# A planned scan layer: numbers per batch, measured durations, paired silus, and six small loads moved to mid-layer

## The chip, the cores and the metric

The kernel runs on one core of a Trainium2 chip, as one launch. The metric is the device time of a launch in microseconds (us). A core has five engines with their own instruction streams: PE (TensorE, matmuls and transposes), DVE (VectorE), ACT (ScalarE, functions from a loaded table), POOL (GpSimd) and SP (SyncE, which here issues nearly all DMAs). Each runs its instructions in order and waits on semaphores for the others. All data is fp32.

## The reference

Two layers, each with a residual, on x of 4 x 512 x 32 x 32 (a batch is 512 channels by 1024 tokens; gn is a group norm with 32 groups):

```
# layer 0, a selective scan over the 1024 tokens of each batch
xn   = layer_norm(gn(x) as tokens x channels) * ln_w + ln_b
xm,z = split(xn @ W_in)                       # 1024 channels each
xs   = silu(causal_conv4(xm) + conv_b)
dt,B,C = split(xs @ W_x); dt = softplus(dt @ W_dt + b_dt)
h[t] = exp(dt[t]*A) * h[t-1] + (dt[t]*xs[t]) * B[t]   # 16 states per channel, A = -exp(A_log)
y[t] = sum over states of h[t]*C[t]
x    = x + ((y + D*xs) * silu(z)) @ W_out
# layer 1, position attention with two 3x3 convolutions
g    = gn(x)
top, center = 1x1 convs(g) with b_top, b_center; bottom = 3x3 conv(g) + b_bottom
m    = softmax over all of (center^T @ top)
x    = x + (3x3 conv(g + m @ bottom) + b_out)
```

## The kernel before

**Tiling of the scan layer.** A batch's 1024 tokens are two halves of 512; its 1024 inner channels are eight chunks of 128 partitions, taken in four pairs. One stretch is a pair and a half (function `delta` makes dt, dt*x and its transpose), and has 16 units, one per state (function `unit`). So a batch has 8 stretches and 128 units, the layer 4 batches and 512 units. One unit, for both chunks of the pair:

- the decay exp(dt*A), on ACT (L862, 128x512 each);
- the input term dt*x*B, in one of two ways. A unit "on ACT" scales rows of the transposed dt*x by B (L875, `sc`, four instructions of 128x256) and PE turns them into PSUM (L901, tile `u`); the decay goes to SBUF (`da`). Otherwise POOL multiplies dt*x by a broadcast B (L890, `dbx`), and the decay goes to `u`;
- the scan over 512 tokens on DVE (L915);
- the product with a broadcast C, on POOL for both chunks at once (L938), or on DVE for each (L931) in some of the units that are not on ACT;
- the sum over states: PE adds the transposed products in PSUM (L948, tile `y`).

After 16 units `gate` multiplies by silu(z) and writes a product to DRAM, and `out_proj` (for the last batch `last_proj`) projects it and adds x. The rows of B and C come as DMAs that broadcast 2 KB to 128 partitions (`bbc`, three buffers; `cbc`, five buffers), issued by SP.

**Which units go where.** `shares` reads two tables: ACT_B, the number of units on ACT in each stretch, and DVE_C, the number that DVE multiplies by C. Each has three rows: batch 0, batches 1 and 2, batch 3.

**What runs in between.** While a batch is scanned, `project_batch` makes the next one ready: `norms` (both norms), `conv1` for each chunk (PE's projection `pxm`, ACT's first tap L667, DVE's other taps L676, then silu on ACT, L685), `params` (dt, B and C). `gates` makes silu(z) (L739). `transform` turns a piece of the second layer's 3x3 weights on POOL (18 pieces, three loads, two scalings on ACT at L1200 and L1201, five kinds of POOL step, twelve stores). Batch 0 is made half by half (`conv1_half`).

**Tables on ACT.** silu, softplus and exp (with log) are in three table sets. A step whose set isn't the loaded one makes ACT load it first (ACT_TABLE_LOAD; for exp it is written at L210).

**What sets the order.** All of this is a list of steps with an engine, an assumed duration, a due time (`prio`, counted in units), what they read, write and hold, and perhaps a table. `Plan.issue` keeps a clock for each engine and always issues the step that could start first, among those within SLACK of it the one due first. A step in another table is held back, by 5.46 table loads, unless it is due well ahead of the rest. HOP and LAG are assumed delays between engines, AHEAD how far past the earliest open due time an engine may go. Due times are numbers in `PRM`: when the projections, gates and pieces fall due. The order so made is the program's order on each engine; the planner's clock has no other effect.

**Ahead of the plan**, in program order: SP loads `gm_sb` and the four chunks of the first x (L294); POOL's queue loads the second layer's `wt_sb` (two DMAs) and `pb_sb` (two); ACT's queue loads `brow_b` and `brow_o`, the second layer's two biases, through a view whose last dimension has stride (L233), and ACT scales them by -12 (L236). Then ACT's queue loads the first layer's small inputs (L315: lnw, lnb, cw, cb, bdt, dp, a_sb), wx and wdt; ACT takes exp of a_sb (L327) and DVE negates it (L328). The first norm is `bn_stats` and `bn_aggr` on DVE (L446, L447), a matmul with gm_sb (L454), small DVE steps, a second matmul (L470), and log and exp on ACT (L479, L484).

**The second layer** (L1324 and later) is written without the planner: scores (L1364, L1385), two 3x3 convolutions as transformed products (L1533), attention (L1585).

Of the kernel before, what the change touches and what calls it, by code (L numbers as in the profile page):

```python
# [8 lines left out]
F32 = mybir.dt.float32  # L9
# [21 lines left out]
PRM = dict(tf=-22.1, pg=0.35, kt=2.5, ke=2.06, ka=-1.93, fl=0, fi=-4.54, m0=42.67, n0=49.76, nl=1.48, q0=67.23, qg=4.59, c0=60.23, cg=6.17, p0=114.55, e0=1.02, eg=7.73, g0=80.83, gg=9.09, o0=14.49, og=6.33, dl=12.15, t0=8, tg=57.65)  # L31


ACT_B = ((12, 9, 10, 9, 9, 10, 9, 9), (11, 9, 12, 8, 9, 8, 8, 8), (9, 9, 12, 12, 11, 12, 12, 13))
DVE_C = ((4, 7, 5, 1, 2, 3, 5, 5), (4, 3, 3, 2, 1, 5, 2, 4), (4, 4, 4, 4, 3, 1, 4, 2))
# [24 lines left out]
class Plan:  # L60
# [4 lines left out]
    LAG = {"PE": 0.2, "DVE": 0.08, "ACT": 0.1, "POOL": 0.06, "SP": 0.0}  # L65
    HOP, LOAD, SLACK, AHEAD = 0.05, 1.3, 0.11, 15.09
# [41 lines left out]
    def issue(self):  # L108
        ready = {e: [s for s in self.steps if s.eng == e and not s.unmet] for e in self.ENGINES}
        clock = {e: 0.0 for e in self.ENGINES}  # L110
# [4 lines left out]
        while left:  # L115
# [4 lines left out]
            for e in self.ENGINES:  # L120
                urgent = min((s.prio for s in ready[e] if s.table in (None, table)), default=1e9)
                found = []
                for s in ready[e]:
                    if s.prio > last:
                        continue
                    t = max(clock[e], s.ready)
                    for b in s.takes:
                        turn = b.free or b.ring not in queues or queues[b.ring][0] is b
                        t = max(t, min(free[b.ring])) if free[b.ring] and turn else 1e9
                    if t >= 1e9:  # L130
                        continue
                    late = s.table not in (None, table)
                    wait = t + (5.46 * self.LOAD if late and s.prio > urgent - 2.66 else 0.0)
                    found.append((wait, s.prio, t, late, s))
# [24 lines left out]
            for b in s.bufs:  # L159
                b.left -= 1  # L160
                if b.ring and not b.left:
                    free[b.ring].append(s.done + self.HOP)
                    if b.done:
                        b.done(b.tile)
            ready[s.eng].remove(s)
            for u in s.users:
                u.unmet -= 1
                other = u.eng != s.eng or s.kb
                u.ready = max(u.ready, s.done + self.HOP if other else clock[s.eng])
# [6 lines left out]
def mamba_then_pab_kernel(  # L176
# [46 lines left out]
    nc.gpsimd.dma_start(wt_sb[:, :, 0, :], w_top.rearrange("(c p) n -> p c n", p=P))  # L223
    nc.gpsimd.dma_start(wt_sb[:, :, 1, :], w_center.rearrange("(c p) n -> p c n", p=P))
    pb_sb = cpool.tile([P, 1], F32, tag="pb", name="pb_sb")
    nc.gpsimd.dma_start(pb_sb[0:PAB], b_top)
    nc.gpsimd.dma_start(pb_sb[PAB:P], b_center)


    brow = []  # L230
    for name, src in (("b", b_bottom), ("o", b_out)):
        t = cpool.tile([1, C], F32, tag=f"brow_{name}", name=f"brow_{name}")
        nc.scalar.dma_start(  # L233
            t.rearrange("o (c p) -> o c p", p=P), src.rearrange("p (c o) -> o c p", o=1)
        )
        nc.scalar.activation(t, t, AF.Copy, scale=-12.0)  # L236
        brow.append(t)
# [46 lines left out]
    with ExitStack() as l0:  # L284
# [7 lines left out]
        first_x = xtp.tile([P, NCC, L], F32, tag="xt", name="xt_0", bufs=1)  # L292
        for c in range(NCC):
            nc.sync.dma_start(first_x[:, c, :], x[0, c * P : (c + 1) * P].rearrange("p h w -> p (h w)"))  # L294

# [6 lines left out]
        def shares(b, n):  # L302

            k = min(b, 1) + (b == B - 1)
            rest = NS - ACT_B[k][n]
            off = [int((i + 0.5) * (NS - 1) / rest) for i in range(rest)]
            c = DVE_C[k][n]
# [20 lines left out]
        nc.vector.tensor_scalar_mul(a_sb, a_sb, -1.0)  # L328
# [39 lines left out]
        MM, TR = 0.88, 0.114  # L368
        ROWS, EXP, SCAN = 0.8, 0.61, 1.18
# [49 lines left out]
        def norms(b, prio, lag=0.0):  # L419

            t = xts[b] = buf("xt", [P, NCC, L], f"xt_{b}")
            if b == 0:
                t.make = lambda: first_x
            src = x[b].rearrange("(c p) h w -> p c (h w)", p=P)
            xin = [buf(None, None, "") for c in range(NCC)]
            step("SP", 0.0, lambda: t(), [], [], prio, holds=[t])
            for c in range(NCC):
                step(
                    "SP", 0.3,
                    lambda c=c: b and nc.sync.dma_start(t()[:, c, :], src[:, c, :]),  # L430
                    [], [xin[c]], prio, kb=512, holds=[t],
                )
# [6 lines left out]
            for c in range(NCC):  # L439
# [9 lines left out]
                step("DVE", 1.4, stats, [xin[c]], [stat], prio, holds=[t])  # L449
# [15 lines left out]
            step("DVE", 0.6, mid, [], [pm, stat], prio)  # L465
# [47 lines left out]
            step("PE", 0.6, shift_mean, [stat], [pv], prio)  # L513
# [61 lines left out]
            for h, (r, pvar) in enumerate(zip(rs, pvars)):  # L575
                at = prio if b else at_half[h]
                step(
                    "ACT", 0.58,
# [74 lines left out]
        def conv1(b, d, prio):  # L653
# [5 lines left out]
            for at, end in ((0, 341), (341, 682), (682, L)):  # L659
# [22 lines left out]
                step("DVE", 0.25 + n * 0.0042, taps, [p], xsh, prio, holds=[u])  # L682
            step(
                "ACT", 1.06,
                lambda: nc.scalar.activation(u(), u(), AF.Silu, bias=cb_sb[:, d : d + 1]),  # L685
                [], xsh, prio, "silu", holds=[u],
# [40 lines left out]
        def gates(b, d, prio):  # L727
# [3 lines left out]
            for h, hs in enumerate(halves):  # L731
                p = project(b, NDC + d, w, f"pz_{b}_{d}_{h}", hs, prio)
                step(
                    "ACT", 0.48,
# [12 lines left out]
        def params(b, prio, hh=tuple(range(NH))):  # L747
# [4 lines left out]
            for n, h in enumerate(hh):  # L752
                hs = halves[h]
                pp = buf("mm" if b or h else "y0", [P, T], f"pp_{b}_{h}")
                for d in range(NDC):
# [7 lines left out]
                        prio + PRM["pg"] * (d + NDC * n) if b else prio - 0.05 * (NDC - d),  # L763
                        holds=[xs[b, k] for k in range(NDC)] if (b or h) and d == 0 else [xs[b, d]],
                    )
                end = prio + (PRM["pg"] * NDC * (n + 1) if b else 0)
                step(
                    "ACT", 0.48,
# [26 lines left out]
        def delta(b, e, h, prio):  # L795
# [5 lines left out]
            for j in range(2):  # L801
# [4 lines left out]
                    "ACT", 0.58,  # L806
# [23 lines left out]
            for j in range(2):  # L830
                pt = buf("mm", [P, NK, P], f"pdt_{name}_{j}")

                def turn(j=j, pt=pt):
# [5 lines left out]
                    "ACT", 0.48, lambda j=j, pt=pt: nc.scalar.copy(dtxt()[:, :, j, :], pt()),  # L839
# [4 lines left out]
        def unit(b, e, h, s, y):  # L844
# [50 lines left out]
            for j, u in enumerate(us):  # L895
                part = parts[j]
                if on_act:
# [11 lines left out]
                    step("PE", 4 * TR, turn, [sc], [u], prio - PRM["kt"])  # L909
                else:  # L910
                    step("ACT", EXP, lambda j=j, u=u: decay(j, u()), [dt], [u], prio - PRM["ke"], "exp")

                def scan(j=j, u=u):
# [10 lines left out]
                    "DVE", SCAN + 0.14 if h == 0 and on_dve else SCAN, scan,  # L924
# [3 lines left out]
                if on_dve:  # L928
                    step(
                        "DVE", 0.6,  # L930
# [3 lines left out]
            if not on_dve:  # L934
                def times_c():
# [5 lines left out]
                    "POOL", 2.31 if h else 2.5, times_c,  # L941
                    [c_bc], [*parts, *([] if h else carry[s])], prio, holds=[hc],
                )
            for j in range(2):
# [8 lines left out]

                step("PE", 4 * TR, add, [parts[j]], [y[j]], prio - PRM["ka"], holds=[hc])

        def gate(b, e, h, y):
# [12 lines left out]
            for j in range(2):  # L969
                step(  # L970
                    "ACT", 0.48, lambda j=j: nc.scalar.copy(yt()[:, j], y[j]()),
                    [y[j]], [yt], prio - 0.5,
                )
            for j in range(2):
# [19 lines left out]
                step("DVE", 1.39, mul, [uh, sz], [p, uh if kept else sz], prio + 2, holds=[u])  # L994
# [111 lines left out]
        def first_image(prio):  # L1106
# [50 lines left out]
            step("DVE", 0.6, mid, [], [pm, stat], prio)  # L1157
# [83 lines left out]
        def project_batch(b):  # L1241

            at = (b - 1) * NDC * NS
            norms(b, at + (PRM["m0"] if b == 1 else PRM["n0"]), PRM["nl"])
            for d in range(NDC):
                when = at + (PRM["q0"] + PRM["qg"] * d if b == 1 else PRM["c0"] + PRM["cg"] * d)
                conv1(b, d, when)
            params(b, at + PRM["p0"])

        norms(0, -20)  # L1250
        for d in range(NDC):
            conv1_half(d, 0, -17 + 0.1 * d)
        params(0, -16, (0,))
        for k in range(NPC + EARLY):
            u, src = ((ub, w_bottom), (uo, w_out))[k // NPC]
            transform(u, src, k % NPC, -5 if k < PRM['t0'] else PRM['tf'] + PRM['tg'] * (k - PRM['t0']))

        LAST = {
            3: (range(4), range(NH), 128 * (B - 1) + 70, 8),
            5: (range(4, 6), range(NH), 128 * (B - 1) + 104, 3),  # L1260
            6: (range(6, NDC), (0,), 128 * (B - 1) + 117, 2),
            7: (range(6, NDC), (1,), 128 * B, 2),
        }
        for b in range(B):
            at = b * NDC * NS
            for n in range(NDC):
                e, h = divmod(n, NH)
                delta(b, e, h, (at + n * NS - PRM["dl"], -15, 9.6)[0 if b else {0: 1, 1: 2}.get(n, 0)])
                if b == n == 0:
                    for d in range(NDC):  # L1270
                        conv1_half(d, 1, -4 + 1.5 * d)
                    params(0, 8.6, (1,))
                if n == 0:
                    for k in range(NDC):
                        gates(b, k, (PRM["e0"] + PRM["eg"] * k, at - 128 + PRM["g0"] + PRM["gg"] * k)[min(b, 1)])
                    if b:
                        for k in range(NH):
                            out_proj(b - 1, k, at + PRM["o0"] + 4 * PRM["og"] * k, PRM["og"])
# [9 lines left out]
        with tc.manual_schedule():  # L1288
            plan.issue()

# [452 lines left out]
```

## Time and profile before

| | us |
|---|---|
| median of 3 runs (lowest, highest) | 2928.78 (2926.93, 2932.84) |
| the profiled execution's own time | 2926.95 |
| its span, first to last instruction | 2925.1 |
| PE busy, all | 2724.9 |
| DVE busy, all | 2292.1 |
| ACT busy, all | 1831.1 |
| POOL busy, all | 2045.6 |
| table loads on ACT: L210 (67), L813 (32), L739 (29), L685 (21), L723 (4) | 1.283 each |

A page of the profile covers one execution. "Busy" is time in which an engine ran instructions; waits, branches and the issuing of DMAs are not counted, and a DMA's issue shows under a queue's name (SPq, ACTq). A group row gives how often a kind of instruction ran, its busy time in all, the mean of one, and the idle time just before it with what ended that. Where instructions overlap in the pipeline, busy time over count is less than the mean of one. A stretch of the timeline gives the start of a row, its length, and in brackets the idle time before it. The granted clock of PE was 0.985 of full speed over the span.

### The profile page before, as it was taken

The page shows a single profiled execution, that of the slowest core. Times are in us where ns is not written, and L with a number is a line of the kernel's source. Part 1 is how long each engine was busy: PE and PEld are TensorE (multiplying, and loading weights), DVE is VectorE, ACT ScalarE, POOL GpSimd, SP SyncE. Part 2 cuts the span into 40 slices and gives each one's busy share as a digit, 9 for nine tenths or more (in the row PEclk, how much of TensorE's full clock was granted, in tenths as well). Part 3 has the DMA queues.
Part 4 walks back from the last instruction along what each step waited for, and adds up shares of the span by engine and source line. Part 5 has one row for each costly group of instructions (what it writes and reads, how often), then busy time and mean ns, then how long its engine had stood idle before and what let it go on. Part 6 is the DMA issues. An engine that isn't in the chain of part 4 may idle for free.

```text
span 2925.1 us, 36166 instructions
## 1 busy us (share of the span) xinstructions
PE 2724.9 (93%) x11712; PEld 1615.4 (55%) x11712; DVE 2292.1 (78%) x2719; ACT 1831.1 (63%) x3248; POOL 2045.6 (70%) x1247
## 2 busy tenths in 40 slices
PE   5988899999899999899999989799999999999998
PEld 2456566666666666666656666544444444444444
DVE  4679899988999989999979999867776655346254
ACT  4689899998799999889998999630200003030000
POOL 6899898899998999998999999733141341214222
PEclk9999899999999999999999999999999999999999
DMA  6856555467545577655567654757789886536487
GB/s 168 235 155 199 165 158 166 152 213 242 195 140 165 172 213 246 200 150 152 175 204 216 219 172 147 160 217 263 256 277 290 307 329 242 200 124 236 162 319 259
DMA packets 405348, 603.94 MB, mean 206 GB/s; under 512 B 46088, under 2 KB 245000, under 8 KB 380584
## 3 DMA queue, kind: packets, MB, share of 16 engines
q1 hardware_dynamic: 396352, 587.11, 62.5%
q10 hardware_dynamic: 8648, 14.26, 1.4%
q8 instruction: 94, 1.54, 0.2%
q14 instruction: 94, 0.77, 0.1%
q0 software_dynamic: 160, 0.26, 0.0%
HBM read 504.53 MB, written 96.99 MB: 206 GB/s over the span
## 4 chain that ended last, share of the span: by engine, by line
PE 34%; DVE 7%; POOL 6%; ACT 5%; issue 3%; DMA 2%; SPq 0%; DVEq 0%; POOLq 0%; ACTq 0%
PE m_o L1533 11%; PE m_b L1533 8%; PE pat L1585 6%; POOL da L938 2%; PE y L948 2%; PE po L412 2%; DVE da L915 2%; PE u L901 1%; ACT sc L875 1%; PE psc L1385 1%; ACT da L862 1%; POOL dbx L890 1%; DMA uw_o<-u_o 1%; POOL dbx L938 1%; DMA u_o<-wr 1%
## 5 line engine op out<-in xcount | busy, mean ns | idle before, releaser
L938 POOL TENSOR_TENSOR da<-da,cbc 128x1024 f32<-128x1024 f32 x313 | 739.9, 2369 | 46.1 <-DVE da L915 32.8
L875 ACT ACTIVATE sc<-dtxt,bt_sb 128x256 f32<-128x256 f32 x1252 | 550.5, 498 | 22.6 <-PE u L901 21.6
L890 POOL TENSOR_TENSOR dbx<-dtx,bbc 128x1024 f32<-128x1024 f32 x199 | 469.9, 2371 | 26.5 <-PE y L948 12.9
L862 ACT ACTIVATE da<-dt,a_sb 128x512 f32<-128x512 f32 x626 | 431.2, 713 | 25.4 <-PE y L948 24.4
L915 DVE TENSOR_TENSOR_SCAN da<-da,u 128x512 f32<-128x512 f32 x328 | 383.8, 1203 | 26.2 <-PE u L901 16.9
L901 PE MATMUL u<-ident,sc 128*128 128x128 f32 x2504 | 363.0, 277 | 34.1 <-DVE da L915 13.8
L948 PE MATMUL y<-ident,da 128*128 128x128 f32 x2504 | 348.8, 279 | 48.9 <-POOL da L938 45.8
L901 PEld LDWEIGHTS u<-ident,sc 128*128 128x128 f32 x2504 | 293.5, 142 | 168.3 <-issue 64.3
L915 DVE TENSOR_TENSOR_SCAN da<-da,carry_sb,u 128x512 f32<-128x512 f32 x298 | 365.2, 1259 | 19.8 <-PE u L901 15.6
L948 PEld LDWEIGHTS y<-ident,da 128*128 128x128 f32 x2504 | 287.7, 143 | 132.3 <-POOL da L938 101.6
L1533 PE MATMUL m_o<-uw_o,v_o 128*128 128x512 f32 x768 | 336.4, 597 | 8.3 <-DMA uw_o<-u_o 8.2
L1533 PE MATMUL m_b<-uw_b,v_b 128*128 128x512 f32 x768 | 333.7, 593 | 4.8 <-ACT e_b L1541 2.2
L862 ACT ACTIVATE u<-dt,a_sb 128x512 f32<-128x512 f32 x398 | 264.9, 681 | 13.9 <-DVE da L915 8.9
L412 PE MATMUL pxm<-xt,winc 128*128 128x345 f32 (+3 forms) x704 | 240.9, 485 | 11.2 <-DMA winc<-in_w_in_dram 4.0
L1533 PEld LDWEIGHTS m_o<-uw_o,v_o 128*128 128x128 f32 x768 | 145.3, 191 | 190.9 <-issue 179.8
L1533 PEld LDWEIGHTS m_b<-uw_b,v_b 128*128 128x128 f32 x768 | 144.9, 190 | 189.9 <-issue 178.9
L412 PE MATMUL pz<-xt,winc 128*128 128x512 f32 x512 | 244.0, 596 | 6.0 <-DMA winc<-in_w_in_dram 2.0
L948 PE MATMUL y<-ident,dbx 128*128 128x128 f32 x1592 | 221.0, 276 | 8.7 <-POOL dbx L938 7.3
L938 POOL TENSOR_TENSOR dbx<-dbx,cbc 128x1024 f32<-128x1024 f32 x93 | 220.6, 2372 | 10.7 <-DMA bbc<-bcd 5.4
L1585 PE MATMUL pat<-y_b,st 128*128 128x512 f32 x512 | 223.3, 597 | 1.6 <-DVE rz L1594 1.6
L948 PEld LDWEIGHTS y<-ident,dbx 128*128 128x128 f32 x1592 | 183.3, 142 | 49.5 <-POOL dbx L938 19.6
L1541 ACT ACTIVATE e_o<-m_o 128x512 f32<-128x512 f32 x24 | 14.3, 597 | 276.8 <-PE m_o L1533 276.8
(229 smaller groups left out, 4259.2 us busy)
## 6 DMA issues: line engine op xcount, KB each, us to landing
cbc<-bcd SPq DMA_DIRECT2D x512, 256.0 KB, 3.7
uw_b<-u_b SPq DMA_DIRECT2D x96, 1024.0 KB, 4.8
uw_o<-u_o SPq DMA_DIRECT2D x96, 1024.0 KB, 4.8
bbc<-bcd SPq DMA_DIRECT2D x199, 256.0 KB, 4.0
u_b<-work SPq DMA_DIRECT2D x192, 128.0 KB, 2.8
winc<-in_w_in_dram SPq DMA_DIRECT2D x72, 256.0 KB, 3.9
szd<-sz SPq DMA_DIRECT2D x32, 512.0 KB, 3.6
szl<-szd SPq DMA_DIRECT2D x32, 512.0 KB, 5.1
```

The lines of the kernel that those rows point to most:

```text
L412: lambda k=k, lhs=lhs, rhs=rhs: nc.tensor.matmul(p()[:, at : at + cols], lhs(), rhs(), start=(k == 0), stop=(k == n - 1)),
L862: nc.scalar.activation(t, dt()[:, j], AF.Exp, scale=a_sb[:, at : at + 1])
L875: nc.scalar.activation(sc()[:, k], dtxt()[:, k], AF.Copy, scale=bt[:, at, s : s + 1])
L890: lambda: nc.gpsimd.tensor_mul(hc(), dtx(), b_bc().to_broadcast([P, 2, T])),
L901: nc.tensor.transpose(u()[:, k * P : (k + 1) * P], sc()[:, k, j, :], ident)
L915: nc.vector.tensor_tensor_scan(ht, *((hc()[:, j], u()) if on_act else (u(), hc()[:, j])), carry_sb[:, j, s : s + 1] if h else 0.0, ALU.mul ...
L938: nc.gpsimd.tensor_mul(hc(), hc(), c_bc().to_broadcast([P, 2, T]))
L948: nc.tensor.matmul(y[j]()[:, k, :], hc()[:, j, k * P : (k + 1) * P], ident, start=(s == 0 and k == 0), stop=(s == NS - 1 and k == NK - 1), ...
L1385: nc.tensor.matmul(pt, top[:, m * P : (m + 1) * P], center[:, h * T : (h + 1) * T], start=True, stop=True,)
L1533: nc.tensor.matmul(m[q], v[:, q, k, c, :], w[:, c, :], start=(c == 0), stop=(c == NCC - 1 and not extra),)
L1541: nc.scalar.activation(e, m[2], AF.Copy, scale=al / 2)
L1585: nc.tensor.matmul(pt, st[m][:, 2 * P * j + h : 2 * P * (j + 1) : 2], xb[m // 2][:, m % 2, :], start=(m == 0), stop=(m == NMC - 1),)
```

## The change

1. The three rows of ACT_B and DVE_C become four, one for each batch, with other numbers, and PRM has values per batch for most due times; the due times of the 18 weight pieces are written out.
2. The planner's assumed durations, hops and lags get other values, hops one per engine; its clocks start at BEGIN instead of zero; the hold on a step in another table goes from 5.46 to 2.11 loads.
3. `silus` becomes a step of its own, for one or two chunks: two in batches 1 and 2, one in batch 3.
4. `wt_sb`, `pb_sb` and the two brows are loaded by a step of SP with due time 300 (a batch is 128), and the brows are scaled after the plan in the program's text, outside its fixed order; in the order that results, these two instructions stand on ACT in the third stretch of batch 2.
5. The first x is loaded by the plan's steps (due at -100); a_sb is negated on ACT.

```diff
-ACT_B = ((12, 9, 10, 9, 9, 10, 9, 9), (11, 9, 12, 8, 9, 8, 8, 8), (9, 9, 12, 12, 11, 12, 12, 13))
-DVE_C = ((4, 7, 5, 1, 2, 3, 5, 5), (4, 3, 3, 2, 1, 5, 2, 4), (4, 4, 4, 4, 3, 1, 4, 2))
+ACT_B = (
+    (12, 8, 10, 9, 10, 8, 8, 8),
+    (11, 8, 12, 9, 8, 9, 8, 8),
+    (11, 9, 13, 9, 10, 8, 9, 9),
+    (9, 11, 12, 12, 10, 13, 12, 14),
+)
+DVE_C = (
+    (3, 5, 6, 3, 1, 3, 5, 6),
+    (4, 7, 2, 3, 3, 5, 2, 5),
+    (5, 4, 3, 1, 5, 6, 3, 6),
+    (4, 3, 3, 4, 6, 1, 3, 1),
+)
...
-    LAG = {"PE": 0.2, "DVE": 0.08, "ACT": 0.1, "POOL": 0.06, "SP": 0.0}
-    HOP, LOAD, SLACK, AHEAD = 0.05, 1.3, 0.11, 15.09
+    LAG = {"PE": 0.17, "DVE": 0.095, "ACT": 0.1, "POOL": 0.06, "SP": 0.0}
+    HOP = {"PE": 0.16, "DVE": 0.045, "ACT": 0.06, "POOL": 0.08, "SP": 0.05}
+    BEGIN = {"PE": 5.0, "DVE": 1.5, "ACT": 9.0, "POOL": 7.0, "SP": 1.5}
+    FREE, LOAD, SLACK, AHEAD = 0.06, 1.3, 0.11, 15.44
+    TURN, URGENT = 2.11, 2.89
...
-                    wait = t + (5.46 * self.LOAD if late and s.prio > urgent - 2.66 else 0.0)
+                    wait = t + (self.TURN * self.LOAD if late and s.prio > urgent - self.URGENT else 0.0)
...
-    nc.gpsimd.dma_start(wt_sb[:, :, 0, :], w_top.rearrange("(c p) n -> p c n", p=P))
-    nc.gpsimd.dma_start(wt_sb[:, :, 1, :], w_center.rearrange("(c p) n -> p c n", p=P))
...
-        nc.scalar.activation(t, t, AF.Copy, scale=-12.0)
-        brow.append(t)
+    def load_l1():
+
+        for k, w in enumerate((w_top, w_center)):
+            nc.sync.dma_start(wt_sb[:, :, k, :], w.rearrange("(c p) n -> p c n", p=P))
+        nc.sync.dma_start(pb_sb[0:PAB], b_top)
+        nc.sync.dma_start(pb_sb[PAB:P], b_center)
+        for t, src in zip(brow, (b_bottom, b_out)):
+            nc.sync.dma_start(
+                t.rearrange("o (c p) -> o c p", p=P), src.rearrange("p (c o) -> o c p", o=1)
+            )
...
-        nc.vector.tensor_scalar_mul(a_sb, a_sb, -1.0)
+        nc.scalar.activation(a_sb, a_sb, AF.Copy, scale=-1.0)
...
-            step(
-                "ACT", 1.06,
-                lambda: nc.scalar.activation(u(), u(), AF.Silu, bias=cb_sb[:, d : d + 1]),
-                [], xsh, prio, "silu", holds=[u],
+        def silus(b, ds, prio):
+
+            def several():
+                for d in ds:
+                    u = xs[b, d]
+                    nc.scalar.activation(u(), u(), AF.Silu, bias=cb_sb[:, d : d + 1])
+
+            step(
+                "ACT", 1.06 * len(ds), several, [], [t for d in ds for t in xh[b, d]], prio, "silu",
+                holds=[xs[b, d] for d in ds],
             )
...
                 conv1(b, d, when)
-            params(b, at + PRM["p0"])
+                if (d + 1) % PRM["xp"][b - 1] == 0:
+                    silus(b, range(d + 1 - PRM["xp"][b - 1], d + 1), when)
+            params(b, at + PRM["p0"][b - 1])

         norms(0, -20)
+        step("SP", 1.6, load_l1, [], [], 300, kb=64)
...
         with tc.manual_schedule():
             plan.issue()
+        for t in brow:
+            nc.scalar.activation(t, t, AF.Copy, scale=-12.0)
```

The rest of the diff is the numbers of PRM (among them xp=(2, 2, 1), the pairing by batch) and the durations handed to `step`, such as SCAN 1.18 to 1.12 or DVE's taps 0.0042 to 0.0037 us per element.

## The prediction

> **What bounds the kernel now.** I read the page's slices first, then the busy time by stretch, cut where the last scan of each batch ends. Those ends I found by laying the planner's order of scans beside the trace: 592, 1042, 1503 and 1883 us. Columns: length, then busy time of PE, its weight loads, DVE, ACT and POOL.
>
> ```profile
> core 0: us, PE busy (x) PEld busy (x) DVE busy (x) ACT busy (x) POOL busy (x), PEclk, DMA share, GB/s
> 0.00:592.00 592.00, 514.72 (x2494) 324.84 (x2495) 483.64 (x607) 506.34 (x872) 508.88 (x357) 0.97 0.59 174
> 592.00:1042.00 450.00, 422.80 (x2300) 288.29 (x2299) 410.95 (x474) 413.80 (x725) 422.38 (x254) 0.98 0.61 188
> 1042.00:1503.00 461.00, 432.06 (x2335) 295.20 (x2334) 413.81 (x477) 424.92 (x741) 435.05 (x267) 0.99 0.61 188
> 1503.00:1883.00 380.00, 344.74 (x2144) 253.40 (x2143) 368.20 (x398) 349.01 (x670) 373.63 (x230) 0.99 0.62 190
> 1883.00:2925.00 1042.00, 1010.61 (x2448) 453.67 (x2446) 615.47 (x766) 137.05 (x242) 305.61 (x143) 0.99 0.71 247
> ```
>
> Four engines are nearly equal in the first layer; POOL is the fullest of the elementwise ones in every batch, and in the last batch it hardly idles (374 of 380). The second layer (last row) is PE's, 1011 of 1042 us, and its code is the same. So the change is worth what it does to the 1883 us ahead of it. There the loss is largest at the start, which the timeline shows (start, duration, engine, line, what; idle time before in brackets):
>
> ```profile
> 0.76 1.26 ACTq L233 DMA_DIRECT2D brow_b<-in_b_bottom_dram  x1
> 2.05 2.44 ACTq L233 DMA_DIRECT2D brow_o<-in_b_out_dram  x1
> 4.52 8.45 ACTq L315 DMA_DIRECT2D lnw_sb<-in_ln_w_dram  x1
> 13.79 1.28 DVE L446 BATCH_NORM_STATS2 bs_l<-xt 128x6 f32<-128x512 f32 x2 [0.62 <-DMA xt<-in_x_dram]
> 14.76 1.35 SPq L1195 DMA_DIRECT2D work<-in_w_bottom_dram  x2
> ...
> 19.69 0.23 DVE L328 TENSOR_SCALAR a_sb<-a_sb 128x128 f32<-128x128 f32 x1 [4.62 <-ACT a_sb L327]
> 19.84 0.20 DVE L447 BATCH_NORM_AGGREGATE mv_l<-bs_l 128x2 f32<-128x12 f32 x1
> 20.09 0.59 PE L454 MATMUL pm_l<-mv_l,gm_sb 128*128 128x4 f32 x2 [20.09 <-DVE mv_l L447]
> ...
> 24.04 0.52 ACT L1200 ACTIVATE work<-work 128x384 f32<-128x384 f32 x1 [4.38 <-DMA work<-in_w_bottom_dram]
> ...
> 26.29 0.27 ACT L479 ACTIVATE gdev_l<-pv_l,eps 128x4 f32<-128x4 f32 x1
> ```
>
> x is there by 13.8 us, yet the first norm goes on at 26.3. Behind the two brow loads lnw's issue takes 8.45 us. Behind that come a_sb, its exp on ACT and its negation on DVE (L328), which stands ahead of the last aggregate. SP's first weight piece also waits for lnw (its queue's waits put 8.4 us down to it), so ACT's L1200, ahead of L479, runs at 24.04.
>
> The rows that cost the edits (count, busy us, mean ns):
>
> ```profile
> L938 POOL TENSOR_TENSOR da<-da,cbc 128x1024 f32<-128x1024 f32 x313 | 739.9, 2369 | 46.1 <-DVE da L915 32.8 <-POOL carry_sb L937 0.2
> L875 ACT ACTIVATE sc<-dtxt,bt_sb 128x256 f32<-128x256 f32 x1252 | 550.5, 498 | 22.6 <-PE u L901 21.6
> L890 POOL TENSOR_TENSOR dbx<-dtx,bbc 128x1024 f32<-128x1024 f32 x199 | 469.9, 2371 | 26.5 <-PE y L948 12.9 <-DMA bbc<-bcd 7.0 <-DVE xs L676 3.4
> L931 DVE TENSOR_TENSOR dbx<-u,cbc 128x512 f32<-128x512 f32 x212 | 138.6, 670 | 0.0
> L685 ACT ACT_TABLE_LOAD x21 | 26.9, 1283 | 0.4
> ```
>
> **The change part by part.** Both kernels can be counted without running, from the order in which the planner issues.
>
> *Shares (ACT_B, DVE_C).* Units that ACT feeds go from 313 to 317 (77, 73, 73, 90 by batch to 73, 73, 78, 93). Those that DVE multiplies by C go from 106 to 121 (32, 24, 24, 26 to 32, 31, 33, 25). POOL loses 4 dbx products and 15 products by C net, 19 x 2.37 = 45 us, and 7 carry copies of 0.19: -46. DVE gains 30 products of 0.65 (138.6/212) and 14 carry copies of 0.16: +22. ACT gains 16 sc of 0.44 (550.5/1252): +7. PE gains 32 transposes of 0.145 (363.0/2504 of L901): +5.
>
> *Silus of two convolutions in one step.* The order holds 141 table loads instead of 153: silu of conv1 21 to 14, of the gates 29 to 26, the rest -2. By the trace one costs 1.28 us, and the next ACTIVATE starts 0.02 us later (98.10 + 1.28, then 99.40): 12 x 1.3 = -15.6 us of ACT. The Trainium skill (ScalarE: Activation LUTs, "What ACT_TABLE_LOAD costs") adds a drain of about 1.38 us and gives 2.66 per switch, which would make -32. The drain would have to stand ahead of the load; there the ACTIVATE ends at 98.09 and the load starts at 98.10. I take the trace. ACT in sum: about -8. A pair also holds the first silu back until the second convolution's taps are done; these xs are for the next batch, a cover of tens of us, and if it were gone params would wait some 5 us once per batch.
>
> *Totals up to the last scan* (order times row): POOL 1739 to 1694, ACT 1694 to 1686, DVE 1676 to 1696, PE 1652 to 1656. The fullest engine falls from 1739 to 1696: -43, if work can move freely over the layer. The fullest by batch is 509, 423, 430, 377 before and 516 (POOL), 420 (DVE), 435 (PE), 369 (DVE) after: 1739 to 1740, no gain, if each batch keeps its idle time. Cut finer, into the 32 stretches of 16 units, the sum of each one's fullest engine goes from 1841 to 1836. Measured is 1883, so neither end is reached. Engines do run ahead over a batch's end (next batch's convolutions, deltas, and up to five loads), and POOL, the one relieved, is the one that idles least; but the other three are close behind. I take half of 43: -21.
>
> *Start.* brow leaves the ACT queue, the negation goes to ACT (+0.3, in its idle time), and SP's first two weight pieces go ahead of x. x then lands at about the same time (0.39 MB more ahead of it, 2.3 us at the slice's 168 GB/s; 0.26 MB of wt and the brow gone). L447 can follow at about 15.5 instead of 20.0, pv 2 us later; ACT's L1200 still stands ahead and now waits for the third piece, behind x and two winc loads, 16 to 18.5 us; table load 1.3; L479 at 18 to 20.5 instead of 26.3. From 46 to 100 us PE is the bound (busy 18 to 19 of every 20 us), and it waits for this chain, so most of it carries on, less a second pair of weight scalings between the first squares. I take -7 (bounds -11 and 0: POOL's pieces may not start earlier).
>
> *Small loads in mid-layer.* Six DMAs are put in SP's queue in the second stretch of batch 2, ahead of the loads of C for unit 0 of the third. The wt and pb loads took 1.06 + 0.80 + 0.58 + 0.54 to issue on POOL, the brows 1.26 + 2.44 on ACT, and whatever stood next 8.45: 15 us for the queue if it repeats. The Trainium skill (DMA: Bandwidth & Descriptors, "Rules for kernel authors") says why and speaks against this place: a last dimension that isn't contiguous becomes one descriptor per element, so each brow's 2 KB are 512 of them, wherever they are issued; sized by bytes alone (260 KB at 188 GB/s) the six would cost 1.4 us. Cover: cbc has five buffers, 5 x 2.9 us = 14.4 (a stretch of 16 units is 46 us), less 3.7 for landing. So 0 to 5 us of bubble on DVE and POOL; on ACT the two scalings of brow now stand between sc and decays of that stretch, some 12 us later, and wait up to 2 if the landing takes the 13 us of the start. I take +4, bounds 0 and 15. At the start the removal is in the -7.
>
> *HOP, LAG, BEGIN, TURN, due times of pieces, projections, gates:* they cost no instruction, they set the order. Their worth is what they do to idle time. The idle rows are many small ones (longest single wait in the four batches 10.1 us), so I can bound it only by POOL's idle outside the start, (592 - 509 - 34) + 28 + 26 + 6 = 109 us: 30 less or 15 more. I take 0 beyond the half above. Second layer: 0.
>
> Sum: -21 - 7 + 4 = -24 on the profiled execution's own 2926.95 (span 2925.1 and 1.85 around it): 2903. The median of the runs stands 1.83 above that execution: 2905.
>
> **The rivals.**
>
> *A, likeliest, 0.50:* the sum above, 2905, its own range 2885 to 2922.
>
> *B, 0.25:* all of POOL's relief arrives, and the order by batch takes a little idle time too: -43 - 7 + 4 - 5 = -51, 2878. For it: batch 3 runs with POOL at 98%, so idle time is not a law. Against: three other engines are within 3% of POOL.
>
> *C, no change, 0.12:* the idle time stays beside each batch's fullest engine (+1), only the start and the small loads count, -2: 2927. For it: 28 and 26 us of POOL idle in batches 1 and 2 while nothing else was full.
>
> *D, slower, 0.13:* the work taken from POOL lands where its new engines are already fullest. Batch 2 gets the extra sc, 43 table loads instead of 38 and 13 us more of PE; its fifth stretch asks 72 us of DVE (66 before) and 68 of ACT (61). If engines can't run ahead over stretches, batches 1 and 2 cost their stretch maxima, +3 and +9, batch 0 POOL's +7 (POOL being its bound, the start's gain is lost too), batch 3 -5: +14, 2943. It decides once those stretches end later than DVE's own load, with POOL idle beside them.
>
> **How the numbers follow.** A measurement of this kernel can tell about 0.2%, 5.9 us, from no change. A and B are faster (0.75), C is within (0.12), D is slower (0.13). The range leaves out the far part of B and of D: 2872 to 2934.
>
> **What would show it.** Right: L479 at 18 to 21 us; POOL's busy time 46 lower and DVE's 22 higher; 12 fewer table loads at 1.28; last scan near 1860; SP's load after brow_o with a long issue and a gap of under 5 us on POOL there. Wrong: L1200 still near 24 us; batch 2 longer than 461 with ACT or DVE nearly full (D); POOL's gaps grown by as much as its work shrank (C); the second layer's 1042 us changed by over 3 us.

## The result, and the profile after

| | before | after |
|---|---|---|
| median of 11 runs each, us (lowest, highest) | 2926.93 (2918.04, 2932.84) | 2914.11 (2908.11, 2918.99) |
| the profiled execution's own time | 2926.95 | 2918.99 |
| its span | 2925.1 | 2917.2 |
| busy PE / DVE / ACT / POOL | 2724.9 / 2292.1 / 1831.1 / 2045.6 | 2728.5 / 2315.5 / 1826.1 / 2001.9 |

The ratio after to before is 0.9955, 95% interval 0.9945 to 0.9966: 13.2 us faster (10 to 16), where 24 were forecast and 2905 for the time (likeliest range 2885 to 2922, in which 2914 lies). The profiled execution of after is the slowest of its 11, 4.9 us above their median; it is 8.0 us under that of before. Below, "against before" comes from ratios of this kind, each made with runs of before on the same chip; 0.001 is 2.9 us. "Against after" divides such a ratio by 0.9955; with the two intervals it is good to 4 or 5 us. The chips differ from run to run, and whether a ratio taken on one chip holds on another was not tested. One execution's last part (the second layer) varies between 1038 and 1051 us over the kernels of this study, none of which touches its arithmetic, so small differences are read from ratios or from stretches, not from one span.

By batch, cut at the last scan of each (the columns are those of the table by batch before: length; busy time and count of PE, PEld, DVE, ACT, POOL; clock; DMA share; GB/s):

```profile
0.00:592.50 592.50, 515.69 (x2449) 326.91 (x2450) 488.88 (x604) 492.49 (x849) 515.09 (x357) 0.96 0.60 175
592.50:1042.20 449.70, 423.44 (x2322) 290.17 (x2321) 419.23 (x491) 405.97 (x716) 408.57 (x246) 0.99 0.61 189
1042.20:1494.30 452.10, 433.20 (x2363) 297.81 (x2361) 424.52 (x506) 431.55 (x756) 404.14 (x247) 0.99 0.64 193
1494.30:1874.40 380.10, 346.89 (x2170) 255.53 (x2168) 367.94 (x398) 359.17 (x694) 366.91 (x226) 0.99 0.61 184
1874.40:2917.20 1042.80, 1009.25 (x2448) 452.17 (x2448) 614.95 (x766) 136.97 (x242) 307.19 (x144) 0.99 0.71 247
```

Only batch 2 is shorter, by 9 us. POOL's work in the four batches fell from 1739.5 to 1694.7, by 44.8, as counted; but the last scan came only 8.1 us sooner (1882.5 to 1874.4, at the finer cut). The other 37 us are new idle time on POOL: 83, 28, 26, 6 by batch before, 77, 41, 48, 13 after.

The start, in the trace's order of time (start, duration, then the instruction):

```profile
0.75 0.39 ACTq L348 DMA_DIRECT2D lnw_sb<-in_ln_w_dram  x1
13.84 1.29 DVE L477 BATCH_NORM_STATS2 bs_l<-xt 128x6 f32<-128x512 f32 x2 [1.03 <-DMA xt<-in_x_dram]
15.16 0.21 DVE L478 BATCH_NORM_AGGREGATE mv_l<-bs_l 128x2 f32<-128x12 f32 x1
...
17.80 0.52 ACT L1237 ACTIVATE work<-work 128x384 f32<-128x384 f32 x1 [5.42 <-DMA work<-in_w_bottom_dram]
20.05 0.26 ACT L510 ACTIVATE gdev_l<-pv_l,eps 128x4 f32<-128x4 f32 x1
```

lnw issues in 0.39 us (8.45 before), the aggregate L478 follows the landing of x at once (15.16; 19.84 before), and the log that ends the first norm, L510 (L479 before), starts at 20.05: 6.24 us sooner. L1237 (L1200 before) still stands ahead of it.

The small loads on SP's queue, in the second stretch of batch 2:

```profile
1139.68 0.76 SPq L273 DMA_DIRECT2D brow_b<-in_b_bottom_dram  x1
1140.48 1.37 SPq L273 DMA_DIRECT2D brow_o<-in_b_out_dram  x1
1142.26 1.00 SPq L892 DMA_DIRECT2D cbc<-bcd  x1
```

From the first of the six (1137.26) to the end of brow_o's issue (1141.85) SP spends 4.6 us. The load of C behind takes 1.00 us, not the 8.45 that stood there at the start; the sign that the prediction had named, a long issue there, did not come.

### The profile page after: what moved, and what is told of

Its sections match the earlier page's. It is cut to its first block, busy times and chain, and to the rows that moved or that the text cites. A ratio compares the mean times of both kernels' runs of the same rounds, so it can differ in the third digit from the quotient of the medians.

```text
span 2917.2 us, 36268 instructions
## 1 busy us (share of the span) xinstructions
PE 2728.5 (94%) x11744; PEld 1622.6 (56%) x11744; DVE 2315.5 (79%) x2762; ACT 1826.1 (63%) x3253; POOL 2001.9 (69%) x1217
## 4 chain that ended last, share of the span: by engine, by line
PE 33%; DVE 12%; ACT 4%; DMA 4%; POOL 3%; issue 2%; SPq 0%; DVEq 0%; POOLq 0%; ACTq 0%
PE m_o L1575 11%; PE m_b L1575 8%; PE pat L1627 4%; DVE da L952 3%; PE y L985 2%; PE po L445 2%; PE u L938 2%; DVE u L952 1%; POOL da L975 1%; ACT sc L912 1%; DVE xs L707 1%; PE psc L1427 1%; ACT da L899 1%; DMA u_o<-wo 1%; DMA uw_o<-u_o 1%
## 5 line engine op out<-in xcount | busy, mean ns | idle before, releaser
L975 POOL TENSOR_TENSOR da<-da,cbc 128x1024 f32<-128x1024 f32 x317 | 749.4, 2370 | 48.3 <-DVE da L952 26.6
L927 POOL TENSOR_TENSOR dbx<-dtx,bbc 128x1024 f32<-128x1024 f32 x195 | 461.1, 2375 | 31.7 <-PE y L985 21.6
L938 PE MATMUL u<-ident,sc 128*128 128x128 f32 x2536 | 374.5, 280 | 50.7 <-DVE da L952 33.1
L952 DVE TENSOR_TENSOR_SCAN da<-da,carry_sb,u 128x512 f32<-128x512 f32 x304 | 372.9, 1261 | 16.5 <-PE u L938 9.5
L985 PEld LDWEIGHTS y<-ident,da 128*128 128x128 f32 x2536 | 294.3, 143 | 85.0 <-POOL da L975 42.1
L899 ACT ACTIVATE u<-dt,a_sb 128x512 f32<-128x512 f32 x390 | 259.3, 682 | 18.8 <-DVE da L952 10.8
L445 PE MATMUL po<-gt,wpr 128*128 128x512 f32 x384 | 182.5, 596 | 1.4 <-PE y L985 0.6
```

Source lines behind the costliest of these rows:

```text
L445: lambda k=k, lhs=lhs, rhs=rhs: nc.tensor.matmul(p()[:, at : at + cols], lhs(), rhs(), start=(k == 0), stop=(k == n - 1)),
L899: nc.scalar.activation(t, dt()[:, j], AF.Exp, scale=a_sb[:, at : at + 1])
L927: lambda: nc.gpsimd.tensor_mul(hc(), dtx(), b_bc().to_broadcast([P, 2, T])),
L938: nc.tensor.transpose(u()[:, k * P : (k + 1) * P], sc()[:, k, j, :], ident)
L952: nc.vector.tensor_tensor_scan(ht, *((hc()[:, j], u()) if on_act else (u(), hc()[:, j])), carry_sb[:, j, s : s + 1] if h else 0.0, ALU.mul ...
L975: nc.gpsimd.tensor_mul(hc(), hc(), c_bc().to_broadcast([P, 2, T]))
```

## The experiments

Twelve kernels. Each kernel keeps the order of the kernel that it is made from, unless its numbers to the planner are changed. Letters name theories within one expectation only. A stretch is named (batch, number), both counted from 0; the scan layer is the first one, up to its last scan.

**b_start: the start alone, in before.** The six small loads become load_l1 as in the change.

```
-    nc.gpsimd.dma_start(wt_sb[:, :, 0, :], w_top.rearrange("(c p) n -> p c n", p=P))
...
-        nc.scalar.dma_start(
-            t.rearrange("o (c p) -> o c p", p=P), src.rearrange("p (c o) -> o c p", o=1)
-        )
...
+        step("SP", 0.0, load_l1, [], [], 300)
...
-        nc.vector.tensor_scalar_mul(a_sb, a_sb, -1.0)
+        nc.scalar.activation(a_sb, a_sb, AF.Copy, scale=-1.0)
```

> The kernel before with the start alone changed: the six small loads of the second layer move to SP's queue in the second stretch of batch 2, the brows are scaled there, a_sb is negated on ACT; shares, due times and durations stay, and so does the order of all else. L479 should start near 20 us instead of 26.3. Theory P (the start carries on, as predicted): the last scan ends 5 to 7 us earlier, -6 us against before. Theory Q (in the first stretches something else ends last, and the start's gain is swallowed there): the first stretch ends within 2 us of 193.6 and the time stays, -1 to 0 us. In both, the small loads cost under 2 us at their new place.

Measured: 2917.11, ratio 0.9979 (0.9969 to 0.999), -6 us. The log of the first norm starts at 19.84 and batch 0 ends at 584.9, 7.2 us sooner. So the start is worth about what the sum gave it (-7), with the six loads in mid-layer included. The trace is less clear: its last scan comes at 1880.1, only 2.4 us sooner than before and not the 5 to 7 of theory P, since stretch (1,6) is 2.2 us longer and (2,0) to (2,4) together as much. (2,1), in which the six loads are issued, and (2,2) last as in before, 49.2 and 46.0 us.

**b_pool38 and a_pool38: 38 half products less on POOL, spread evenly.** 38 of the POOL products by C do one of their two chunks only (the other chunk is left unmultiplied); in after it is 38 of 391.

```
-    nc.gpsimd.tensor_mul(hc(), hc(), c_bc().to_broadcast([P, 2, T]))
+    cut[0] += 38
+    if cut[0] >= 406:
+        cut[0] -= 406
+        nc.gpsimd.tensor_mul(hc()[:, 0], hc()[:, 0], c_bc()[:, 0])
+    else:
+        nc.gpsimd.tensor_mul(hc(), hc(), c_bc().to_broadcast([P, 2, T]))
```

> The kernel before, its order unchanged; 38 of its 406 products by C on POOL, spread evenly, are made for one chunk only (the other chunk's product by C is left out), which takes 38 x 1.19 = 45 us off POOL and nothing off the other engines. Theory P (half of a relief of POOL arrives): -20 us. Theory Q (PE, with 515, 423 and 432 of 592, 450 and 461 us, is as full as POOL in batches 0 to 2, so a relief of POOL becomes idle time of POOL): -3 to -8 us, nearly all of it in batch 3, where POOL is 98% busy and gets 10 us of the relief.

> The kernel after, its order unchanged; 38 of its 391 products by C on POOL made for one chunk only (the other's product is left out): another 45 us off POOL. Theory P: another -15 to -20 us against after. Theory Q: -0 to -4 us, since POOL now idles 41 and 48 us in batches 1 and 2.

Measured: b_pool38 2913.07, ratio 0.9963 (0.9948 to 0.9978), -10.8 us; a_pool38 2907.49, ratio 0.9944 (0.9932 to 0.9957), about -3 against after, where the two intervals overlap. A half product takes 1.28 us and a whole one 2.37, so POOL's busy time fell by 41 and 42 us, not by the 45 expected (the same holds for b_hit and b_miss below). In before, 41 us less of POOL, put nowhere else, bring a quarter of it, between theories P and Q, and not mainly in batch 3, which is 2.1 us shorter in the trace; in after, less still.

**b_hit and b_miss: the same 38 half products, but placed.** They go into 15 stretches in which POOL is the fullest engine of before (b_hit, the first table), or into nine in which it is not (b_miss, the second). Keys are batch and stretch, values the number of half products.

```
+    at = (b, 2 * e + h)
+    seen[at] = seen.get(at, -1) + 1
+    half = seen[at] % 2 == 1 and seen[at] < 2 * CUT.get(at, 0)
...
+    CUT = {(1, 1): 3, (1, 2): 3, (1, 7): 3, (2, 0): 3, (2, 2): 3, (2, 3): 3, (2, 4): 3, (2, 7): 3,
+           (2, 1): 2, (3, 0): 2, (3, 1): 2, (3, 2): 2, (3, 3): 2, (3, 4): 2, (3, 5): 2}
...
+    CUT = {(0, 3): 4, (0, 5): 4, (0, 7): 4, (1, 0): 4, (1, 5): 4, (1, 6): 4, (2, 6): 4,
+           (0, 6): 5, (2, 5): 5}
```

> The kernel before, in its own order, with 38 of its 406 POOL products by C done for one of the two chunks only (so POOL works about 45 us less), all 38 in 15 stretches of 16 units in which POOL is the fullest engine in the trace of before (two or three in each of (1,1) (1,2) (1,7), (2,0) to (2,4), (2,7), (3,0) to (3,5)). Theory F (relief counts where POOL is the fullest engine of its stretch, up to its lead over the second): the leads of these stretches in the trace of before, each capped at what is cut, add up to 14.5 us; some of it goes to waits: 7 to 14 us faster, ratio 0.995 to 0.9976. Theory G (what counts is POOL's total up to the last scan, wherever it is cut): as the same 45 us spread over all stretches gave, 10.8 us, ratio about 0.9963. This run alone tells little; its partner b_miss decides.

> The kernel before, in its own order, with the same 38 POOL products by C cut to one chunk (45 us less of POOL), but all in nine stretches in which another engine is the fullest in the trace of before: (0,3), (0,5), (0,6), (0,7), (1,0), (1,5), (1,6), (2,5), (2,6). Theory F (only the fullest engine of a stretch counts): within 3 us of before, ratio 0.999 to 1.001. Theory G (POOL's total up to the last scan counts): about 11 us faster, ratio 0.996, as for b_hit.

Measured: b_hit 2913.3, ratio 0.9965 (0.9951 to 0.9978), -10.2 us; b_miss 2919.39, ratio 0.9986 (0.9977 to 0.9995), -4.1 us. By these medians the same POOL time is worth two and a half times as much where POOL leads; the intervals just touch, so the factor itself is not well known. By the traces the last scan comes 16.0 us sooner in b_hit and 10.0 in b_miss, 11.4 and 5.8 of it in the cut stretches. G, which asks for the same from both, is out of favour; F's 0.999 for b_miss is just missed. Two stretches show it, (2,5) and (3,0), one table for each kernel. Before:

```profile
core 0: us, PE busy (x) PEld busy (x) DVE busy (x) ACT busy (x) POOL busy (x), PEclk, DMA share, GB/s
1324.00:1385.40 61.40, 60.35 (x312) 41.01 (x311) 60.10 (x73) 59.06 (x100) 51.11 (x24) 1.00 0.54 164
1502.80:1550.10 47.30, 41.23 (x244) 29.78 (x243) 43.83 (x54) 42.62 (x74) 46.46 (x31) 0.96 0.79 248
```

b_miss, which cuts in the first of the two:

```profile
1313.20:1374.60 61.40, 60.30 (x312) 41.01 (x310) 60.06 (x72) 59.06 (x100) 45.59 (x24) 1.00 0.53 166
1491.90:1539.20 47.30, 41.28 (x244) 29.60 (x243) 43.84 (x54) 42.64 (x74) 46.47 (x31) 0.96 0.78 248
```

b_hit, which cuts in the second:

```profile
1314.30:1375.70 61.40, 60.36 (x312) 41.02 (x310) 60.12 (x73) 59.07 (x100) 51.03 (x24) 1.00 0.55 163
1493.10:1538.60 45.50, 39.58 (x244) 28.69 (x243) 43.75 (x53) 42.42 (x74) 44.16 (x31) 1.00 0.81 256
```

In (2,5) PE and DVE are busy for 60 of 61.4 us. POOL falls from 51.11 to 45.59, and the stretch lasts 61.40 all the same. In (3,0) POOL has 46.46 of 47.30; it falls by 2.3, and the stretch by 1.8. Over all cut stretches of b_miss, seven of nine repeat their length within 0.1 us; the other two are (0,3), -4.0, of which 2.2 also come in b_hit where nothing was cut there, and (1,6), -1.8. In b_hit the cut stretches are 11.4 us shorter in sum, 6.3 of it in batch 3 and 2.7 in (2,3). In the five that did not shorten ((1,7), (2,0), (2,1), (2,4), (2,7)) POOL led the second engine by 0.8 us or less. But a small lead is not a ceiling: in (3,1) to (3,5) POOL led by less than 0.5, and they became 0.5 to 1.4 us shorter. The sum does better than the single stretch. Worked out from the trace of before, with each lead capped at what is cut, it is 14.5 for b_hit and 12.4 for the even spread of b_pool38, which were 10.2 and 10.8 us faster.

**a_pz, a_dve, a_act: which engine after feels.** One each of: one of the four matmuls of every gate projection left out (56 us less in the rows of pz, 36 in PE's busy time); three of four DVE products by C on half of their columns (DVE 48 less); silu of z and its table loads left out (ACT 60 less, where 65 were expected).

```
-    lambda k=k, lhs=lhs, rhs=rhs: nc.tensor.matmul(
+    lambda k=k, lhs=lhs, rhs=rhs: (name.startswith("pz_") and k == 1) or nc.tensor.matmul(
...
-    lambda j=j, u=u: nc.vector.tensor_mul(hc()[:, j], u(), c_bc()[:, 0]),
+    lambda j=j, u=u, n=T if (b + 2 * e + h + s) % 4 == 0 else T // 2: nc.vector.tensor_mul(
+        hc()[:, j, :n], u()[:, :n], c_bc()[:, 0, :n]
+    ),
...
-    "ACT", 0.97, lambda: nc.scalar.activation(sz(), sz(), AF.Silu),
+    "ACT", 0.97, lambda: None,
```

> The kernel after, its order unchanged; of the four matmuls that add up a projection of the gates (pz) one is left out (a quarter of the sum over channels is missing): 64 x 0.87 = 56 us off PE, in batches 0 to 2 (19 us each and less in batch 3). Theory Q (PE ends last in batches 0 to 2): -15 to -30 us against after, spread over batches 0 to 2. Theory P (POOL and ACT bound these batches): under -8 us.

> The kernel after, its order unchanged; in 3 of 4 units that DVE multiplies by C, only half of the columns are multiplied (the product is missing on the rest): about 181 x 0.27 = 48 us off DVE. Theory R (in batches 0 to 3 no engine ends last for long; four engines hand on to each other with short waits, and a relief of any of them arrives to a tenth to a quarter): -4 to -12 us against after. Theory S (DVE, which got 23 us more, is what bounds the order now): -25 us or more, with batch 3, where it is busy 368 of 380, shorter by over 5.

> The kernel after, its order unchanged but for ACT's missing instructions: silu(z) is left out (the gate multiplies by z itself), and with it 24 table loads: 32 x 1.06 + 24 x 1.28 = 65 us off ACT. Theory R: -6 to -16 us against after. Theory T (ACT bounds the order, and table loads are what holds the others up): -30 us or more.

Measured: a_pz 2911.56, ratio 0.9954 (0.994 to 0.9967), nothing against after. a_dve 2902.59, ratio 0.9929 (0.9915 to 0.9944), -7.6 against after. a_act 2918.18, ratio 0.9974 (0.9966 to 0.9982), 5.5 *slower* than after. So by the ratios no engine is the bound of after: the best of four reliefs returns 16% of what it takes out.

The traces read otherwise in part. Scan layer and second layer of a_pz, then of a_act (columns as in the tables by batch):

```profile
0.00:1864.70 1864.70, 1678.69 (x9168) 1145.44 (x9168) 1699.69 (x1996) 1688.22 (x3011) 1693.03 (x1074) 0.98 0.61 185
1864.70:2911.20 1046.50, 1014.08 (x2448) 454.57 (x2448) 615.27 (x766) 137.04 (x242) 307.05 (x144) 0.99 0.71 246
0.00:1869.50 1869.50, 1713.96 (x9296) 1171.82 (x9296) 1700.59 (x1996) 1629.60 (x2955) 1693.15 (x1074) 0.98 0.62 185
1869.50:2914.50 1045.00, 1013.53 (x2448) 454.34 (x2448) 615.09 (x766) 137.03 (x242) 306.17 (x144) 0.99 0.72 246
```

In after the scan layer ends at 1874.4; here it ends 9.7 and 4.9 us sooner, in a_dve 18.3, in a_pool38 9.1. About 3 us of each lie in (1,1), where the trace of after was long (60.6, in these four 57.2 to 57.5); that execution of after is the slowest of its 11. The second layer, whose code is the same, took 3.7 and 2.2 us longer than in after. So the scan layer of a_act is not slower in the trace, and no stretch of it is over 1.7 us longer than in after: where its 5.5 us come from stays open.

The reliefs also limit the stretch view. In the trace of after PE is the fullest engine of 11 stretches and ACT of 10. Worked out as for b_hit, with each lead capped at what PE's busy time fell by, they add up to 14.7 us for PE in a_pz; by the ratio nothing came, by the trace these 11 stretches are 7.5 us shorter, 3.1 of it in (1,1). PE's busy time fell by 36 us where 56 us of its rows were left out, so it is not a fixed demand, and for PE "fullest" says less.

**a_b0: after with before's due times for the start of batch 0.**

```
-    d1=8.23,
+    d1=9.6,
...
-    h0=-5.26,
-    hg=2.44,
-    p1=2.25,
-    d2=-9.17,
+    h0=-4,
+    hg=1.5,
+    p1=8.6,
+    d2=19.85,
```

> The kernel after with the due times of batch 0's start as before (second halves of the convolutions at -4 and 1.5 apart, their projection to dt, B and C at 8.6, the deltas of the second and third stretch at 9.6 and 19.85); the rest of the new numbers stays, and the order differs from after in batch 0 alone. Theory U (the start's gain is given back because the new due times finish the second halves late, so that the second stretch's first scan waits 7.6 us at 193 to 201): the second stretch ends near 242 instead of 248, batch 0 near 585, -6 us against after. Theory V (batch 0 loses elsewhere, by the shares): the time stays within 2 us of after.

Measured: 2921.7, ratio 0.9991 (0.998 to 1.0002), about 10 us slower than after: stretch (0,1) lasts 59.2 (55.0 in after, 49.9 in before). Its trace has 4.0 of the 10, at the last scan. Neither theory came true. That these due times had cost after its early start is thereby wrong; the other numbers of after need them.

**a_shares and b_shares: the tables of shares exchanged.** After with ACT_B and DVE_C of before, and before with those of after, each planned anew. ACT_B of a_shares is shown, its rows put one to a line; DVE_C likewise, and b_shares the other way round.

```
-    (12, 8, 10, 9, 10, 8, 8, 8),
-    (11, 8, 12, 9, 8, 9, 8, 8),
-    (11, 9, 13, 9, 10, 8, 9, 9),
-    (9, 11, 12, 12, 10, 13, 12, 14),
+    (12, 9, 10, 9, 9, 10, 9, 9),
+    (11, 9, 12, 8, 9, 8, 8, 8),
+    (11, 9, 12, 8, 9, 8, 8, 8),
+    (9, 9, 12, 12, 11, 12, 12, 13),
...
```

> The kernel after with ACT_B and DVE_C as before (planned anew with the new numbers and durations): POOL gets its 45 us back, DVE loses 22. If the shares carry part of the gain: +5 to +11 us against after (a relief of POOL of the same size was worth 10.8 in the order of before). If the new order carries it: 0 to +3.

> The kernel before with the tables of shares (ACT_B, DVE_C) of after, planned anew with all of before's due times, costs and rules: the same relief of POOL as the change has (its work up to the last scan 1739 to 1694 us), nothing else of it. Theory G (totals count): 21 us faster, ratio 0.993, as the prediction's largest term had it. Theory F (the fullest engine of each stretch, summed: 1840.9 to 1840.5): no change, ratio 0.999 to 1.001. Theory T (shares and due times are a set, as the opposite mixture showed with 57 us): slower by 10 to 50 us, ratio 1.003 to 1.017.

Measured: a_shares 2979.26, ratio 1.0188 (1.0165 to 1.0211), 68 us slower than after, far outside what was expected. b_shares 2967.9, ratio 1.0148 (1.0131 to 1.0165), 43 us slower than before, as theory T had it, although POOL is busy for 2002.1 us as in after (2001.9), 43.5 less than in before. Batches 0, 1 and 3 lose 15, 12 and 12 us, stretch (2,4) lasts 81.2 instead of 69.2. In a_shares a single wait of DVE for PE is 17.6 us long. The columns are engine, line, who is waited for, us in all, times, longest:

```profile
DVE pyb L1015 <- PE pyb L1008: 17.6, 1, 17.6
```

**a_nopair: after with each silu a step of its own.**

```
-    xp=(2, 2, 1),
+    xp=(1, 1, 1),
```

> After with the silus of each convolution a step of their own again (batches 1 and 2), planned anew, all else as in after: 7 more table loads on ACT, 9 us at the 1.28 us of the trace. Theory P (the pairs save their loads on the path): 3 to 9 us slower than after, ratio 0.9965 to 0.9986 against before. Theory O (the pairs only lie beside other work, ACT being the fullest in a third of the stretches): within 3 us of after, ratio 0.9945 to 0.9965. By the sum of the fullest engine of each stretch (1836.2 to 1829.3) it would be up to 7 us faster than after, ratio 0.993.

Measured: 2927.32, ratio 1.0013 (1.0006 to 1.002), 17 us slower than after: more than either theory said. The trace has 148 table loads (141 in after) and ACT is busy 9.9 us longer. Its last scan is at 1883.4, 9.0 later than in after. Of the stretches that grew, (0,5), where batch 1's silus lie, has 5.7 us more of ACT and is 4.8 longer. But (1,3) is 9.6 longer and (2,4) 4.3, with no more ACT, since the planner put the steps in another order ((1,4) is 5.1 shorter). So the pairs and the order made for them are worth 17 us together; how much is the loads alone was not separated.

No kernel that does all of the work was faster than after.

## Why the prediction was right and wrong

The direction held, and the time lies in the likeliest range, but the sum was nearly double what came, and that its sign held is in part luck. By the traces nothing of the gain stands in batch 0, where the start's 7 was to be (592.1 and 592.5), and 8.7 us of it stand in batch 2, where the prediction saw the danger (rival D). The last scan was to come near 1860 and came at 1874.4.

*Start, -7: right in size, but not where it was expected.* Alone it is worth 6 us by the ratio (3 to 9), 2.4 at the last scan by the trace (b_start), and L510 at 20.05 lies in the 18 to 20.5 of the sum. In after it is gone again by the end of batch 0: the first stretch ends at 193.3 (193.6 before) though its first scan starts at 102.0 instead of 119.4, and (0,1) lasts 5.1 us longer. Where that stretch begins, DVE stands still for the second half's projections, for their transpose `pbt` and then for `dbx`, which is made from the `dt` that they yield:

```profile
189.72 0.23 DVE L828 COPY bt_sb<-pbt 128x64 f32<-128x64 f32 x1 [5.41 <-PE pbt L820]
190.96 2.33 DVE L952 TENSOR_TENSOR_SCAN da<-da,u 128x512 f32<-128x512 f32 x2 [1.01 <-ACT da L899]
200.91 2.47 DVE L952 TENSOR_TENSOR_SCAN u<-u,carry_sb,dbx 128x512 f32<-128x512 f32 x2 [7.62 <-POOL dbx L927]
```

*Small loads, +4: too high.* They take 4.6 us of SP, but in b_start the stretch that holds them and the next are not longer than in before (49.2 and 46.0), so no cost of theirs shows there. The trace of the start was the nearest row, but its 8.45 us did not come with the loads.

*Shares, "I take half of 43: -21": this is the step that failed.* The counts were right: POOL -43.7 and DVE +23.4 over the span, where -46 and +22 were forecast. Wrong was what they are worth. With 24 forecast and 13.2 measured, of which the start has 6 by itself, about 7 remain for the shares, the pairs and the order together (good to 4), where the sum had 17. The sum had three gauges, -43 for the whole layer, -5 for the 32 stretches and +1 for the batches, and went to the middle of the widest, since "engines do run ahead over a batch's end". By the traces they do so too little: the sum over the stretches of the fullest engine's busy time is 1800.7 before and 1794.7 after: -6, beside a last scan 8.1 sooner. The group rows of after show the relief itself, as counted:

```profile
L975 POOL TENSOR_TENSOR da<-da,cbc 128x1024 f32<-128x1024 f32 x317 | 749.4, 2370 | 48.3 <-DVE da L952 26.6
L912 ACT ACTIVATE sc<-dtxt,bt_sb 128x256 f32<-128x256 f32 x1268 | 554.6, 497 | 35.4 <-PE u L938 34.4
L927 POOL TENSOR_TENSOR dbx<-dtx,bbc 128x1024 f32<-128x1024 f32 x195 | 461.1, 2375 | 31.7 <-PE y L985 21.6
```

and b_hit against b_miss supports the view that its place counts. That the stretch sum is only half a rule, a_shares and a_nopair show: by their traces it is 1826.4 and 1794.2, 31.7 above after and the same as in after, while the last scan comes 57.8 and 9.0 us later. It does not see waits that a new order makes.

*Order at 0: wrong in kind.* The prediction priced order, HOP, due times and pairs at nothing beyond the half. b_shares puts numbers on them: with after's shares but before's due times and costs the kernel is 43 us slower than before, with all of after 13 faster. So the numbers belong together: the start could be had alone, the shares could not. In these runs they pay only with the order made for them.

*Table loads:* 12 fewer, at 1.283 us, as counted; ACT's busy time fell by 5.0 (forecast 8). Of the 140 loads of after behind the first, 133 stand without a gap of 0.1 us on either side, so the drain that the prediction left out does not show.

*The rivals.* B (2878) falls: even relief without any new work for DVE gives 11 of 41 us. C's sign came: 37 of POOL's 45 us turned into idle time; it was wrong in the rest, and the result is clear of no change. D's sign did not come. Its stretch did: (2,4) was to ask 72 us of DVE, and it lasts 72.4 with DVE busy for 71.4 (69.2 before). But (2,0), (2,3) and (2,7) became 5.4, 6.2 and 8.5 us shorter, POOL having been their fullest engine before, so batch 2 ended up 8.7 shorter.

## What to carry to other kernels

In a pipeline where every engine is near full, price a relief by stretch: where the relieved engine leads, up to its lead over the second fullest; elsewhere at little (b_miss: 4 of 41 us by the ratio, the interval 1 to 7). In before this came near for POOL in sum, though not stretch by stretch; in after it failed for PE. An engine's total over a layer said little here, since the fullest engine changes from one stretch to the next. Where shares and due times go into one planner, treat them as one set and price the set from the order that it makes; half of such a set was slower than either whole one, by 43 to 68 us.

## What was not expected of the hardware

- The slow issue behind element-wise loads is not a property of the loads alone. At the start, on ACT's queue, the two brow loads took 1.26 and 2.44 us and the DMA behind them 8.45; in mid-layer, on SP's, 0.76, 1.37 and 1.00. Whether the queue or the moment makes the difference was not separated.
- Where the order is the same, most stretches repeat to a tenth of a microsecond over kernels and executions: (2,5) is 61.4 in before, b_hit, b_miss, b_start; (1,4) is 72.7 in after, a_b0, a_pool38, a_pz and a_act. A few vary, those in which even the fullest engine idles: (0,3), 67.8 in before and 65.6 in b_hit, and (1,1), 60.6 in after and 57.2 to 58.3 in the five kernels that keep its order there. So one profile is enough to judge most stretches.
- With 60 us of ACT's work taken out, after was 5.5 us slower by the ratio, though its scan layer ended 4.9 us sooner in the trace. No cause was found.
